# Layer 2's ends: where the recheck's branch stands, when rows are reloaded, and how far ahead pieces are requested

## The chip, the cores and the metric

The kernel runs on one core of a Trainium2 chip. The metric is device microseconds of one execution; a run's time is given beside the median of three runs. The profile is of one execution, taken by the hardware profiler. Its engines are PE (TensorE matmuls), PEld (TensorE weight loads), DVE (VectorE), ACT (ScalarE), POOL (GpSimd) and SP (SyncE, which here only issues DMAs and keeps order). PEclk is the TensorE clock that was granted, 1.00 being full speed.

## The reference

A graph network of four layers on 4096 nodes with 256 features and a random 0/1 adjacency `adj`; each layer is added to its input and normalised.

```python
x = ln(x + gat(x))                       # layer 0: attention over the edges, 8 heads
x = ln(x + (diag(adj) + adj) @ x @ W)    # layer 1
# layer 2, two steps on Xf = Xa = x:
R = rownorm(adj + eye)
for n in range(2):
    A = top_p_attention(Xa, p=0.9)       # softmax of q.k, only each row's nucleus, renormalised
    Xf, Xa = R @ Xf, A @ Xa
    Z = Z + Xf @ U1[n].T + Xa @ U2[n].T
x = ln(x + ln(x + Z) * g + b)
agg = adj @ x / max(deg, 1)              # layer 3
x = ln(x + relu(concat([x, agg]) @ W + b))
```

The nucleus of a row is the smallest set of its largest probabilities whose sum reaches 0.9. The layer's end in layer 2 holds two normalisations, one of its own and the residual one.

## The kernel before, in words

The 4096 nodes are 32 blocks (`NB`) of 128 rows. In layer 2 each of the two steps runs a loop over blocks 0 to 30, written out by hand (`tc.manual_schedule` keeps the order of the five engines as issued), with eight slots `s` in each block. A slot does one eighth of the block's attention product: `turn` (L1297, PE transposes of the masked scores), a copy to `aT` by ACT (L1299), and `gather` (L1306, eight matmul rows). Between the slots stand the pieces of other blocks' work: the scores of block b+2 (L935), DVE's nucleus of block b+1, and `diffusion`, the product R @ Xf of block b+2 (step 0) or b+3 (step 1). That product reads the adjacency in pieces of 256 KB, `adj_piece`, of which there are three buffers; SP requests them (L176) and PE multiplies each by the rows `XD` in four matmuls (L179). Every helper is a generator, and the loop's `next(...)` says where its next part goes.

When a step has no diffusion left (from block 30 in step 0, 29 in step 1), `XD` is no longer needed there. Then two things happen at the step's end:

- `reload` (L1153) brings the next operation's rows into `XD`, 1 MB for four blocks, on SP's queue. In step 0 these are the rows of the second diffusion, in step 1 the rows of layer 3.
- `early` (L1504 the matmuls, L1495 the piece's request) begins the next operation's products beside the last gathers: 21 pieces of blocks 0 to 2 in step 0, 35 pieces of blocks 0 to 4 of layer 3 in step 1. The order of the pieces is the list `todo`. In step 1 a piece on the diagonal gets the identity taken off by POOL (L1497). `made` records the products done.

A cheap nucleus is used, with a check: `settled` (L1186 to L1219) computes for each block whether the cheap cut was exact (`row`, with the minimum over all blocks as a flag); it ends in a DMA of `row` to memory (L1218, on SP's queue). Every engine loads the flag (`values_load`, L1690 in step 0, L1735 in step 1), and `mend` (L1155 to L1181) is a branch on it (L1159) whose body, the exact computation, is skipped here. In step 0 it stands in front of block 31's gather; in step 1 behind it, after the last `closing`'s first operation.

`store` (step 0) writes a block's result; `closing` (step 1, L1450 to L1467) scales it on ACT, adds the rest and runs both normalisations, mostly on POOL, and writes `xo`. `ahead3` (L1469) prepares the block's rows for layer 3 and writes them to `xtd`, from where `reload` takes them.

The tail of step 1, from block 31's gather on, holds the last closing, the reload of the last rows, the remaining pieces (`beside`), the last piece of each of the blocks 0 to 4, and `product(0..3)` (L1743), the whole product of block 5, whose pieces are casts into `kT` from the adjacency as bytes (`nad`, loaded by `load_bytes`, L1780, 1 MB a load). The bytes come in two sets of buffers: `nas` (in the score tiles `es[2]` and `es[0]`) and four tiles in `X`.

Layer 3 then goes over blocks 6 to 31. `ready(b)` casts the block's bytes to fp32r in eight-block pieces (`cast3`, L1790 on DVE, L1792 on ACT), `products(b)` is 32 matmuls (L1823), and `close(b)` (L1829 to L1839) is the mean, residual and normalisation. The six blocks that layer 2 began, `early3`, need only `close`.

## Time and profile before

| what | value |
|---|---|
| median of three runs | 4086.25 us (4081.27, 4086.25, 4087.33) |
| the profiled execution's own time | 4083.41 us |
| its span, first to last instruction | 4081.7 us |
| PE busy | 3911.8 us, 96% of the span |
| DVE busy | 2996.7 us, 73% |
| ACT busy | 2758.5 us, 68% |
| POOL busy | 1078.4 us, 26% |
| mean granted clock | 0.983 |
| last gather of step 1 done | 3832.1 us |
| last matmul of layer 2 done | 3872.2 us |

A timeline row gives the start, the length, the engine and line, the operation with its tiles, how many instructions were merged, and in brackets the engine's idle time before it with what released it. A row of waits gives the engine and line that waited, what it waited for, the sum in us, how often, and the longest. A "q" behind an engine's name is its sequencer. A window row gives the stretch, its length, then busy time of PE, PEld, DVE, ACT and POOL with the number of instructions, the granted clock, the busy share of the DMA engines and GB/s.

### The profile page before, as it was taken

The numbers are of one execution on the slowest core, as the hardware profiler recorded it, in microseconds if no ns is written. First come the engines' busy times: TensorE is split into PE (matmuls) and PEld (weight loads), VectorE is DVE, ScalarE is ACT, GpSimd is POOL, SyncE is SP. The second block draws the span as 40 slices with busy tenths as digits, with TensorE's granted clock in tenths as the row PEclk, the third lists the DMA queues.
The fourth block names the chain that finished last, engine by engine and source line by source line (L and its number), as shares of the span: only waits on it lengthen the run. The fifth ranks groups of instructions, "written<-read, shape, count | busy, mean of one in ns | idle before, by whom it ended". The sixth has DMA issues, their size and how long they took to land. (4 is left out here: it accounts for less than half of the span.)

```text
span 4081.7 us, 68719 instructions
## 1 busy us (share of the span) xinstructions
PE 3911.8 (96%) x25081; PEld 3381.4 (83%) x25081; DVE 2996.7 (73%) x6647; ACT 2758.5 (68%) x5127; POOL 1078.4 (26%) x1318
## 2 busy tenths in 40 slices
PE   7999989999999799799999999999999999999899
PEld 6899989999999688468888888865888888887677
DVE  7642329999999444548778787837899999999264
ACT  5543329999998322458888888825988888887132
POOL 0111110110333122301111111114555555555211
PEclk9999999999999999899999999999999999999999
DMA  4765555324221597433232332463333333335441
GB/s 119 230 211 176 179 178 186 96 85 143 76 89 43 205 380 281 120 106 99 97 102 92 100 97 95 140 196 99 109 108 103 118 103 105 119 100 204 163 150 47
DMA packets 291194, 555.90 MB, mean 136 GB/s; under 512 B 38966, under 2 KB 115382, under 8 KB 286742
## 3 DMA queue, kind: packets, MB, share of 16 engines
q1 hardware_dynamic: 208676, 394.61, 29.1%
q0 software_dynamic: 27664, 84.44, 6.2%
q10 hardware_dynamic: 54498, 72.27, 5.1%
q8 instruction: 203, 3.33, 0.3%
q14 instruction: 153, 1.25, 0.1%
HBM read 385.25 MB, written 165.94 MB: 135 GB/s over the span
## 5 line engine op out<-in xcount | busy, mean ns | idle before, releaser
L1306 PE MATMUL ps_a<-X,aT 128*128 128x256 f32 x4096 | 972.8, 380 | 1.3 <-ACT h L1447 1.1
L1306 PEld LDWEIGHTS ps_a<-X,aT 128*128 128x128 f32 x4096 | 775.8, 190 | 128.3 <-issue 3.6
L300 PE MATMUL acc<-gm,gt 128*128 128x198 bf16 x8192 | 704.2, 248 | 26.1 <-issue 14.9
L300 PEld LDWEIGHTS <-gt 128*128 128x128 fp8e4 x8192 | 700.3, 97 | 29.9 <-issue 15.1
L292 ACT ACTIVATE sg<-lpb,nlc 128x1024 fp8e4<-128x1024 f32 x640 | 671.4, 1135 | 59.6 <-DVE gt L294 34.4
L179 PE MATMUL ps_r<-XD,adj_piece 128*128 128x512 f32 x1952 | 548.5, 415 | 9.7 <-DMA adj_piece<-adjs 9.6
L517 PE MATMUL pz<-src,ar 128*128 128x264 f32 x4096 | 508.3, 287 | 11.9 <-DVE ar L507 9.8
L517 PEld LDWEIGHTS pz<-src,ar 128*128 128x128 f32 x4096 | 505.2, 189 | 14.8 <-DVE ar L507 13.6
L1028 ACT ACTIVATE ja<-e,nc 128x2048 uint8<-128x2048 f32 x240 | 480.9, 2004 | 2.0
L1299 ACT COPY aT<-ps_tp 128x512 f32<-128x512 f32 x512 | 296.4, 579 | 232.9 <-PE ps_tp L1297 230.8
L179 PEld LDWEIGHTS ps_r<-XD,adj_piece 128*128 128x128 f32 x1952 | 345.2, 189 | 85.4 <-DMA adj_piece<-adjs 13.9
L510 ACT ACTIVATE nb<-a 128x512 uint8<-128x512 f32 x256 | 156.8, 630 | 292.2 <-DMA a<-in_adjt_dram 289.8
L1093 DVE MAX8 cand<-v 128x8 f32<-128x256 f32 x1024 | 347.2, 412 | 4.4
L1143 DVE SCALAR_TENSOR_TENSOR e<-e,edge 128x512 f32<-128x512 f32 x512 | 347.3, 749 | 2.2
L1297 PE MATMUL ps_tp<-ident,e 128*128 128x128 f32 x2048 | 308.8, 274 | 2.1 <-DVEq L1159 2.1
L1089 DVE SCALAR_TENSOR_TENSOR v<-e,hi 128x2048 f32<-128x2048 f32 x128 | 301.4, 2355 | 2.4
L1297 PEld LDWEIGHTS ps_tp<-ident,e 128*128 128x128 f32 x2048 | 257.8, 142 | 54.2 <-issue 3.7
L935 PE MATMUL ps_logit<-kT,q 128*128 128x512 f32 x1024 | 277.6, 413 | 9.9 <-DVE kT L893 5.7
L285 DVE TENSOR_SCALAR sg<-lpb,nlc 128x1024 fp8e4<-128x1024 f32 x384 | 283.0, 773 | 2.0
L937 ACT ACTIVATE e<-ps_logit 128x1024 f32<-128x1024 f32 x256 | 260.1, 1026 | 30.7 <-PE ps_logit L935 29.6
L507 DVE CAST ar<-a 128x1024 fp32r<-128x1024 f32 x128 | 88.7, 693 | 232.0 <-PE pz L517 231.9
L731 PE MATMUL ps_adj<-XD,adj_piece 128*128 128x512 f32 x1024 | 236.1, 391 | 0.0
(382 smaller groups left out, 5501.1 us busy)
## 6 DMA issues: line engine op xcount, KB each, us to landing
adj_piece<-adjs SPq DMA_DIRECT2D x552, 256.0 KB
a<-in_adjt_dram SPq DMA_DIRECT2D x256, 256.0 KB
adjs<-adj_piece SPq DMA_DIRECT2D x96, 512.0 KB
na<-nad SPq DMA_DIRECT2D x64, 512.0 KB
nad<-nb POOLq DMA_DIRECT2D x128, 128.0 KB, 3.4
lpb<-lpd POOLq DMA_DIRECT2D x32, 512.0 KB, 4.1
na<-nad ACTq DMA_DIRECT2D x16, 1024.0 KB
gmd<-gb ACTq DMA_DIRECT2D x64, 198.0 KB
```

What stands on the lines that cost most here:

```text
L179: nc.tensor.matmul(ps, a[:, k, :], rhs(jc).rearrange("p s d -> p (s d)"), start=(jc == 0), stop=(jc == self.NB - 1))
L285: nc.vector.tensor_scalar(sg[:, k, :], lpb, nlc[:, jc, h:h + 1], 2.0 ** -5, op0=ALU.is_ge, op1=ALU.mult, saturate=False)
L292: nc.scalar.activation(sg[:, k, :], lpb, AF.Sign, scale=-1.0, bias=nlc[:, jc, h:h + 1], saturate=False)
L300: nc.tensor.matmul(acc[:, q, :6 * C1], gt[:, k, q * P:(q + 1) * P], gm[:, jc, hh, :], start=(jc == 0 and q % 2 == 0), stop=(jc == NB - 1 a ...
L517: nc.tensor.matmul(pz[q][:, t, :W], ar[:, q, k, :], src[:, jc, t, s], start=(jc == 0 and s == 0), stop=(jc == NB - 1 and s == 1))
L1028: nc.scalar.activation(ja, e[:, s * HALF:(s + 1) * HALF], f, bias=nc1, accum_out=fs[:, i + s:i + s + 1])
L1089: nc.vector.scalar_tensor_tensor(v, ec, hi, ec, op0=ALU.is_lt, op1=ALU.mult, accum_out=sb[:, s:s + 1])
L1093: nc.vector.max(cand[:, 8 * j:8 * j + 8], v[:, k * 256:(k + 1) * 256])
L1143: nc.vector.scalar_tensor_tensor(ec, ec, edge[:, j:j + 1], ec, op0=ALU.is_ge, op1=ALU.mult)
L1297: nc.tensor.transpose(pt[:, k * P:(k + 1) * P], e[:, jc * P:(jc + 1) * P], self.ident)
L1299: nc.scalar.copy(aT, pt)
L1306: nc.tensor.matmul(pa[:, :D], aT[:, k * P:(k + 1) * P], X[:, jc, :], start=(jc == 0), stop=(jc == NB - 1))
```

## The change

There are five parts.

1. In step 1 the branch (`values_load` of the flag and `mend`) stands in front of block 31's gather, as in step 0, and both steps share the code. `closing` loses its parameter `hand`. So that the row is there, the last parts of `settled` and of block 31's nucleus come in slots 6 and 7 of block 30, not after the loop. The row's DMA goes to ACT's queue. In step 0 the rest of blocks 0 to 2 of the next diffusion (last reload, last pieces, `diffused`, `keep`) follows the branch in the code; in the built order two of its three piece requests move behind the branch on SP, its reload does not.
2. The reloads of `XD` are given a slot each, by the table `freed` (key: block counted from the end of diffusion, slot): in step 0 slots 4 to 7 of the last block with diffusion and slots 0, 2 and 4 of the next; in step 1 over three blocks. Before, five came in slots 3 to 7 of one block (in step 1 in its slots with a piece), one or two straight behind it and one, in step 1, a block later.
3. `early` holds two requested pieces, not one, and requests the first two straight behind the last diffusion.
4. In step 1 the tiles `nas` are made and their four loads asked for behind the branch. The two of them into `es[0]`, which stood in front of the branch in the built order, move behind it; the two into `es[2]` stand in front of it in both. The four loads into `X`, which `ready(8)` asks for in the code of before and which stand amid the tail's pieces in its built order, are requested behind the last piece (`load_bytes(rows, 1, 0)`); `reload(xtd, NB - 4, NB - 1)` comes behind `whole(beside)`.
5. In layer 3 the casts of blocks 6 and 7 come first, and the six early closes are spread, one behind each of `products(6)` to `products(11)`, in the order 2, 5, 0, 1, 3, 4.

```diff
-            def mend(step, row, flag, e, r, h=None, made=()):
-
-
-                spare = es[(NB - 2 + step) % 3][:, :N]
+            def mend(step, row, flag, e, r, made=()):
+
+
+                spare = es[(NB - 2) % 3][:, :N]
                 with tc.If(flag == 0):
...
                     with tc.If(nc.values_load(row[:, NB - 1:NB], min_val=0, max_val=1) == 0):
-                        if step == 1:
-                            e2, Z = exact_scores(NB - 1, spare)
-                            r2 = exact_nucleus(e2, Z)
-                            nc.scalar.mul(h[:, 0], attention(e2)[:, :D], r2)
-                        else:
-                            e2, Z = exact_scores(NB - 1, e)
-                            nc.vector.tensor_copy(r, exact_nucleus(e2, Z))
+                        e2, Z = exact_scores(NB - 1, e)
+                        nc.vector.tensor_copy(r, exact_nucleus(e2, Z))
                     if step == 1:
...
                 nc.vector.tensor_reduce(row[:, NB:], pt[:1, :NB], AX.X, ALU.min)
-                nc.sync.dma_start(rowd, row)
+                nc.scalar.dma_start(rowd, row)
                 return rowd
...
-            def closing(b, pa, r, xb, hand=None, queue=nc.scalar):
+            def closing(b, pa, r, xb, queue=nc.scalar):
...
                 nc.scalar.mul(hb, pa[:, :D], r)
-                if hand:
-                    hand(h)
-                    yield
                 nc.gpsimd.tensor_add(hb, hb, xb[:, 0])
...
-                a = piece(step, *todo[0])
+                held = [piece(step, *t) for t in todo[:2]]
+                yield
                 started = set()
                 for i, (b, g) in enumerate(todo):
-                    after = piece(step, *todo[i + 1]) if i + 1 < len(todo) else None
-                    times(banks[b], a, g, b not in started)
+                    if i + 2 < len(todo):
+                        held.append(piece(step, *todo[i + 2]))
+                    times(banks[b], held.pop(0), g, b not in started)
                     made.append((banks[b], b, g, b not in started))
                     started.add(b)
-                    a = after
                     yield
...
                 banks, made = {}, []
+                freed = ((-1, 4), (-1, 5), (-1, 6), (-1, 7), (0, 0), (0, 2), (0, 4)) if step == 0 else \
+                    ((0, 4), (-1, 5), (-1, 6), (-1, 7), (0, 0), (0, 2), (1, 1))
+                freed = {at: g for g, at in enumerate(freed)}
                 if step == 0:
...
                             beside = diffusion(step, b + dd)
-                        elif b + dd == NB:
-                            beside = early(step, todo, banks, made)
                         if step == 0 and not ahead:
...
                             pieces = (1, 2, 2, 2, 2, 2, 1, 1)
-                        close, kept, put, difs, count = None, None, None, None, 0
+                        close, kept, put, difs = None, None, None, None
                         for s in range(8):
...
                                 next(beside)
-                                if b + dd == NB - 1 and count > 2:
-                                    reload(rows_of, 4 * count - 12, 4 * count - 8)
-                                count += 1
+                            if (b + dd - NB, s) in freed:
+                                g = freed[b + dd - NB, s]
+                                reload(rows_of, 4 * g, 4 * g + 4)
                             gather(pa, aTs.pop(0), s)
...
                                 aTs.append(turn(es[(b + 1) % 3], s - 6))
-                            if s == 1 and step == 1 and not ahead:
-                                reload(rows_of, NB - 8, NB - 4)
+                            if s > 5 and not ahead:
+                                if s == 6:
+                                    next(row)
+                                    next(edge)
+                                else:
+                                    row = result(row)
+                                    rs[b + 1] = whole(edge)
                         if b + dd < NB:
...
                         if b + dd == NB - 1:
-                            reload(rows_of, NB - 12, NB - 8 + 4 * (step == 0))
+                            beside = early(step, todo, banks, made)
+                            next(beside)
...
                         banks.update({3: pl[:, 0], 4: pl[:, 1]})
-                    next(row)
-                    next(edge)
-                    next(beside)
-                    row = result(row)
-                    rs[b] = whole(edge)
-                    for _ in range(3 if step == 0 else 5):
-                        next(beside)
+                    r = rs.pop(b)
                     if step == 0:
-                        reload(rows_of, NB - 4, NB)
-                        sums = [base(1, 0), base(1, 1)]
-                        for k in range(3):
-                            times(banks[k], piece(0, k, 7), 7)
-                            if k == 2:
-                                sums.append(base(1, 2))
-                            whole(diffused(1, k, banks[k], sums[k]))
-                            whole(keep(1, k, sums[k]))
-
-                r = rs.pop(b)
+                        store(b - 1, pa, rs.pop(b - 1))
+                        whole(beside)
+                    else:
+                        close = closing(b - 1, pa, rs.pop(b - 1), xc)
+                        next(close)
+                        for _ in range(6):
+                            next(beside)
+
+                flag = nc.values_load(row[:, NB:], min_val=0, max_val=1)
+                mend(step, row, flag, es[b % 3][:, :N], r, made[:] if step else ())
                 if step == 0:
-                    flag = nc.values_load(row[:, NB:], min_val=0, max_val=1)
-                    store(b - 1, pa, rs.pop(b - 1))
-                    mend(step, row, flag, es[b % 3][:, :N], r)
+                    reload(rows_of, NB - 4, NB)
+                    sums = [base(1, 0), base(1, 1)]
+                    for k in range(3):
+                        times(banks[k], piece(0, k, 7), 7)
+                        if k == 2:
+                            sums.append(base(1, 2))
+                        whole(diffused(1, k, banks[k], sums[k]))
+                        whole(keep(1, k, sums[k]))
                     pa = ps1.tile([P, 512], F32, name="ps_a")
...
-                nas = [t[:, i * 2048:(i + 1) * 2048].bitcast(U8).rearrange("p (k i) -> p k i", k=8)
-                       for t in (es[2], es[0]) for i in range(2)]
                 with tc.manual_schedule(engines=five):
+                    nas = [t[:, i * 2048:(i + 1) * 2048].bitcast(U8).rearrange("p (k i) -> p k i", k=8)
+                           for t in (es[2], es[0]) for i in range(2)]
                     self.load_bytes(nas, 0, 0)
                     xb = bases(b)
-                    close = closing(b - 1, pa, rs.pop(b - 1), xc)
-                    next(close)
                     h = done.pop(b - 2)
...
                             xT = turned(h[:, 0], bank())
-                    hand = []
-                    close = closing(b, pa, r, xb, hand.append)
-                    next(close)
-                flag = nc.values_load(row[:, NB:], min_val=0, max_val=1)
-                mend(step, row, flag, None, None, *hand, made[:])
-                with tc.manual_schedule(engines=five):
+                    close = closing(b, pa, r, xb)
                     ps = ps1.tile([P, 512], F32, name="ps_a")
...
                         next(beside)
-                    reload(xtd, NB - 4, NB - 1)
                     next(close)
                     whole(beside)
+                    reload(xtd, NB - 4, NB - 1)
                     lasts = []
...
                         lasts += [two[:, 0], two[:, 1]]
+                    rows = [X[:, 8 * i:8 * i + 8, :].rearrange("p b d -> p (b d)").bitcast(U8)
+                            .rearrange("p (k i) -> p k i", k=8) for i in range(4)]
                     product(0)
...
                         nc.tensor.matmul(to, t, XD[:, b].rearrange("p s d -> p (s d)"), start=False, stop=True)
-                self.ahead3 = nas, [X[:, 8 * i:8 * i + 8, :].rearrange("p b d -> p (b d)").bitcast(U8)
-                                    .rearrange("p (k i) -> p k i", k=8) for i in range(4)]
+                    self.load_bytes(rows, 1, 0)
+                self.ahead3 = nas, rows
                 self.early3 = [banks[k] for k in range(5)] + [ps]
...
                 it = b * P // self.IT
-                if b * P % self.IT == 0:
+                if b * P % self.IT == 0 and it > 1:
                     self.load_bytes(nas[it % 2], it, 0)
...
             ready(6)
-            for b, ps in enumerate(self.early3):
-                if b == 5:
-                    ready(7)
-                close(b, ps)
+            ready(7)
+            rest = [2, 5, 0, 1, 3, 4]
             for b in range(6, NB):
...
                     ready(b + 2)
+                if rest:
+                    k = rest.pop(0)
+                    close(k, self.early3[k])
                 close(b, ps)
```

## The prediction

> **What bounds the kernel now.** I read the table of windows first, because a share over the whole span mixes stages; it gives each stretch's length, the busy time of PE, PEld, DVE, ACT and POOL, the granted clock, the DMA share and GB/s.
>
> ```profile
> 2695.00:2712.00 17.00, 11.26 (x37) 8.17 (x38) 3.79 (x12) 2.44 (x4) 2.75 (x4) 0.70 0.52 171
> 3200.00:3600.00 400.00, 400.00 (x1972) 332.36 (x1971) 384.08 (x957) 351.90 (x842) 223.90 (x263) 1.00 0.34 110
> 3715.00:3732.00 17.00, 14.21 (x63) 11.13 (x62) 13.92 (x31) 10.22 (x31) 3.18 (x6) 0.90 0.96 362
> 3762.00:3795.00 33.00, 28.87 (x129) 23.05 (x128) 25.07 (x80) 4.45 (x9) 16.07 (x19) 0.90 0.59 191
> 3830.00:3855.00 25.00, 14.71 (x48) 10.22 (x47) 1.22 (x4) 4.37 (x5) 6.27 (x9) 0.83 0.76 265
> ```
>
> In the middle of step 1 PE is busy 400.00 of 400 us at clock 1.00, with DVE close behind (384.08). There nothing can be won, and the change leaves it alone. At the ends PE has holes and the clock falls: 11.26 busy of 17 at 0.70, 14.71 of 25 at 0.83. So the change can win at most those holes and the half-clock work after them.
>
> Next the early products' own line, with what ended PE's idle time before it, then PE's timeline at the holes (start, length, matmuls in the row, idle before and its releaser).
>
> ```profile
>   DMA adj_piece<-adjs: 40.0, 27
>   POOL adj_piece L1497: 11.0, 4
> ```
> ```profile
> 2698.81 1.43 PE L1504 MATMUL ps_logit<-XD,adj_piece 128*128 128x512 f32 x4 [2.79 <-DMA adj_piece<-adjs]
> 2700.03 1.91 PE L1504 MATMUL ps_r<-XD,adj_piece 128*128 128x512 f32 x4
> 2704.01 0.66 PE L1297 MATMUL ps_tp<-ident,e 128*128 128x128 f32 x2 [2.07 <-DVEq L1159]
> 3726.95 3.54 PE L1306 MATMUL ps_a<-X,aT 128*128 128x256 f32 x8
> 3773.78 1.65 PE L1504 MATMUL ps_logit<-XD,adj_piece 128*128 128x512 f32 x3 [3.07 <-POOL adj_piece L1497]
> 3840.20 3.44 PE L1504 MATMUL ps_logit<-XD,adj_piece 128*128 128x512 f32 x8 [4.62 <-DMA adj_piece<-adjs]
> 3848.40 1.20 PE L1504 MATMUL ps_logit<-XD,adj_piece 128*128 128x512 f32 x4 [1.86 <-DMA adj_piece<-adjs]
> 3874.08 11.44 PE L1823 MATMUL ps_tp<-XD,adj_piece 128*128 128x512 f32 x48 [1.88 <-DVE adj_piece L1790]
> ```
>
> Pieces that land late are the largest cause. Eight gather matmuls take 1.89 us elsewhere (the row at 3721.29) and 3.54 at 3726.95: a hole costs twice, once idle and once at half clock.
>
> Last, SP's waits near the end of step 1 (total, times, longest), and who waited for the branch in both steps:
>
> ```profile
> SPq L1495 <- PE ps_logit L1504: 52.3, 27, 5.9
> SPq L1159 <- SPq L1159: 19.1, 6, 6.5
> SPq L1218 <- DVE row L1217: 5.8, 1, 5.8
> ```
> ```profile
>   POOL h L1458: 13.1, 1
>   DVE v L848: 5.8, 1
>   PE ps_tp L1297: 2.1, 1
> ```
>
> SP, which alone requests pieces, stands in PE's shadow (a buffer must come free) and for 19.1 us in the branch. The branch costs PE 2.1 us in step 0, but POOL 13.1, which is idle time off the path.
>
> **The change, part by part.** The sum is made against the profiled run, 4083.41 us (span 4081.7). The median, 4086.25, is 2.84 above it; I take the saving off the median.
>
> *End of step 0* (reloads spread, pieces two ahead). PE waits for pieces at 2643.28, 2653.44, 2663.05, 2698.81 and 2705.56: 1.23 + 2.17 + 0.60 + 2.79 + 0.88 = 7.67. Half clock after them, from rows such as 1.91 against 1.18 for four matmuls: 2.8. Gross 10.5. In before, five 1 MB reloads go out in one block, on the queue of the pieces. A piece issued alone is used about 2.4 us after its issue, one behind a reload 5 to 7 (issued 3845.07, used 3852.42). With one reload every two slots (about 7 us, while 1 MB moves in some 3 to 4 at 265 to 362 GB/s) the queue should empty between. A reload can still hit one piece, and SP now requests the last two pieces behind the branch, not in front of it (2.4 us bare at worst, turns beside it): I keep back 1.5. The branch stays at its place, its 2.07 with it. **Net 9.0**, bounds 4 (the stalls of the first two rows only move) and 12 (the join shrinks too).
>
> *Blocks 28 to 30 of step 1* (the same, and two ahead). Idle 0.22 + 0.27 + 2.30 + 1.06 + 3.07 = 6.92; half clock 3.54 − 1.89 = 1.65, then 3.37 − 1.89 = 1.48 at 3775, and 0.7 at 3773.78, together 3.83. Gross 10.75. Of it the 3.07 is POOL: its diagonal addition L1497 (0.45) stood behind L1462 of the layernorm (2.75). A piece requested one earlier passes POOL before that. I keep back 1.75. **Net 9.0**, bounds 4 and 10.75.
>
> With three buffers the request of a piece waits in either kernel for the release of the piece three before it. So "two ahead" moves its place in the queues of SP and POOL, and hides no more than that. That is the ground of the first rival.
>
> *Mask, row and branch of step 1 in front of the gather.* Removed: idle 0.80 (3800.14) and 2.05 (3803.15, POOL's addition taking 2.84 beside DVE instead of 0.46), and half clock 2.9 behind them (eight transposes, four weighted products, a piece): 5.7. Added: a join of five engines with work left on PE. It queues PE's 64 gather matmuls with their transposes, ACT's copies aT and POOL's layernorm behind it, and two 1 MB loads of bytes on SP. Step 0 has that join and PE paid 2.07. Row and flag come by the same chain: the store of row, about 1 us to the loads (2695.72 to 2696.8), a load of 0.46 to 1.95, a branch of 0.05 to 0.07. Before it the last six pieces of `early` give PE some 5.6 us of cover (24 matmuls at 0.235); without them the chain's 3 to 4 us would be bare. The row's store on ACT's queue frees SP from 4.3 and 5.8 us of waiting; I credit it inside these terms. **Net 3.0**, nearest to step 0's row; bounds 0 and 5.
>
> *Tail, last gather to layer 3.* Before: gather done at 3832.1, layer 2's last matmul at 3872.2: 40.1 us. Idle 0.45 + 4.62 + 0.24 + 0.30 + 1.86 + 2.82 + 1.33 + 0.77 = 12.39; half clock 3.26 (3.44 − 2.12, 2.08 − 1.19, 3.14 − 2.09). Together 15.65; the rest, 24.4, is work. The cause: 4 MB of bytes for X are requested amid the pieces, between 3834.6 and 3859.2, and all SP work starts only when it leaves the branch at 3834.5. After, the branch is past and the X loads come behind the last piece. Two pieces fewer are left (8 matmuls, 1.9 us), but that work is only moved and counts for nothing. What is late next: the reload of 0.75 MB and the last pieces behind it, 3 us, which I keep back with 0.15 for the rest. **Net 12.5**, bounds 8 (pieces at the one-queue cadence of 2.4 us each) and 15.65.
>
> *Start of layer 3.* Idle 1.88 + 0.77 + 2.96 = 5.61 (casts behind closes) and half clock 9.27 − 7.47 = 1.8; gross 7.4. Two casts first remove the later two; the first cast still waits for the last block's xo store (issued 3869.92, cast at 3873.29), and the X loads now move beside it: keep 3.4. The closes, one per block, cost DVE about 2.7 each: 4.0 + 2.7 = 6.7 of 7.47 us per block, so they hide; uncovered, six would be 16. **Net 4.0**, bounds 1 and 5.
>
> Sum 9.0 + 9.0 + 3.0 + 12.5 + 4.0 = 37.5. One tenth (3.5) goes for stalls that no row of before shows: **34**, bounds 17 and 48. 4086.25 − 34 = **4052 us**; the ends are 4069 and 4038.
>
> **A rule against the rows.** Half clock makes 2.8 + 3.8 + 2.9 + 3.3 + 1.8 = 14.6 of my gross sum. The trace has it after single holes of 2.30 (3726.95) and 2.79 us (2700.03). The Trainium skill, "TensorE: Matmul & The Clock Gate", "Why this matters for your kernels", warns only of gaps over about 3 us. By it, only what follows the 3.07 and 4.62 holes would be throttled, 0.7 + 1.48 + 1.32 = 3.5, and the saving would be some 11 us smaller, about 23. The rows decide here.
>
> Moving the row's store to ACT's queue meets another one. The Trainium skill, "DMA: Bandwidth & Descriptors", "Issuing engines are not separate DMA queues", says that another issuing engine saves only issue time. By it this edit is worth next to nothing; SP's 5.8 us row is waiting and not transfer, so the two are not in conflict.
>
> **The rivals.** *Transfers bind still* (0.22): L1495's 52.3 us on PE in 27 waits says that a buffer, not the order, releases requests, and 362 GB/s at share 0.96 in the window at 3715 says that bytes limit there. Then each end keeps its bytes and stalls only move. Saved: 3 of step 0, 3 of blocks 28 to 30, 1.5 at the branch, 7.5 in the tail (X loads out of the way), 4 in layer 3: 19, so **4067**. Against it: the window after that one runs at 0.48.
>
> *The join holds all engines* (0.11): SP sat in step 1's branch from 3815.1 to 3834.6, 19.5 us. If that is the join's own price, and PE pays it now in both steps with 5 us half clock each, 2 × 24.5 = 49 stands against 34: +15, **4101**. It decides from 17 us of join per step. Against it: the last engine arrived at 3832.1 (ACT) and SP left 2.4 us later, so SP was waiting for the others.
>
> *Savings are given back* (0.07): the four X loads, now last, reach layer 3 late; 8 blocks' casts wait 4 us each, 32 of the 34 lost: **4084**. Against it: block 8, the first to use X, lies two blocks of 7.47 us behind the first product.
>
> **How the numbers follow.** Forecast 0.60, rivals 0.22, 0.11 and 0.07. A measurement of this kernel can tell about 0.2% (8 us) from no change. Forecast and the first rival lie wholly beyond that: faster 0.82; the third is within it: 0.07; the second slower: 0.11. The range 4038 to 4072 takes the forecast's bounds and the first rival with 5 us to spare, and leaves out 0.18.
>
> **What would show it.** Right: windows at both ends with PE over 95% busy and clock over 0.95; L1504's successor (L1496) waiting under 20 us for pieces and POOL; from the last gather to layer 3 about 26 us; the branch's PE wait under 3 us in both steps; the first layer 3 rows without holes after the first. Wrong: a PE idle of over 5 us released by the branch's engines, pieces still at 5 to 7 us between issue and use, or DVE as the releaser of PE in blocks 6 to 11 of layer 3. If the time falls and the holes stay, my places are wrong though the sum is not.

## The result and the profile after

The changed kernel took 4073.24 us (median of 7, 4066.64 to 4075.74) beside 4083.97 us of the kernel before (median of 7, 4081.27 to 4087.33). The ratio is 0.9971, 95% interval 0.9959 to 0.9983: faster, by 11 us and not by 34. Another five runs on a later occasion gave 4067.74, beside 4083.31 of before. The time lies above the range's upper end, 4072; the sign was right and the size was not.

The table of windows of the changed kernel, at the stretches shown of before and at the one that now holds the branch (length; busy PE, PEld, DVE, ACT, POOL; clock, DMA share, GB/s):

```profile
2695.00:2712.00 17.00, 13.34 (x60) 9.66 (x59) 4.98 (x14) 2.22 (x4) 1.02 (x2) 1.00 0.66 206
3762.00:3795.00 33.00, 32.88 (x159) 26.68 (x158) 30.00 (x88) 6.80 (x17) 15.43 (x20) 1.00 0.55 182
3795.00:3812.00 17.00, 11.23 (x37) 7.52 (x36) 3.40 (x8) 2.02 (x4) 5.96 (x7) 0.81 0.51 162
3830.00:3855.00 25.00, 18.66 (x65) 12.41 (x63) 1.22 (x4) 4.26 (x5) 6.29 (x9) 0.90 0.59 181
```

Block 30 of step 1 is full (32.88 of 33). The window with the branch is emptier than it was (11.23 of 17 at 0.81; before 14.15 at 0.80), and the tail is better but still a hole (18.66 of 25). What PE waited for in front of the early products, then PE's timeline at the holes that are left:

```profile
  DMA adj_piece<-adjs: 34.6, 27
  POOLq L1159: 4.3, 2
```
```profile
2673.24 1.20 PE L1496 MATMUL ps_logit<-XD,adj_piece 128*128 128x512 f32 x4 [1.79 <-DMA adj_piece<-adjs]
2686.89 2.07 PE L1496 MATMUL ps_logit<-XD,adj_piece 128*128 128x512 f32 x4 [3.22 <-DMA adj_piece<-adjs]
2704.52 2.11 PE L1496 MATMUL ps_logit<-XD,adj_piece 128*128 128x512 f32 x8 [2.85 <-DMA adj_piece<-adjs]
3798.77 4.62 PE L1496 MATMUL ps_logit<-XD,adj_piece 128*128 128x512 f32 x12 [1.95 <-POOLq L1159]
3808.32 0.41 PE L1385 MATMUL ps_tp<-ident,h 128*128 128x128 f32 x2 [3.52 <-PEq L1159]
3848.59 0.96 PE L1496 MATMUL ps_logit<-XD,adj_piece 128*128 128x512 f32 x3 [2.31 <-DMA adj_piece<-adjs]
3869.48 16.71 PE L1817 MATMUL ps_tp<-XD,adj_piece 128*128 128x512 f32 x64 [1.95 <-DVE adj_piece L1784]
```

The waits for pieces fell from 40.0 to 34.6 only. In step 0 each of the three holes stands behind one reload: these are the rows of the reloads on SP's queue, and the piece behind each starts on PE 6 to 9 us later.

```profile
2666.89 0.43 SPq L1153 DMA_DIRECT2D XD<-xfd  x1
2678.88 1.40 SPq L1153 DMA_DIRECT2D XD<-xfd  x1
2695.43 0.38 SPq L1153 DMA_DIRECT2D XD<-xfd  x1
```

The 3.52 us at 3808.32 are new. The 1.95 at 3798.77 are not: before, PE waited 2.05 us for POOL at the same point of the program (3803.15), and the forecast took that wait to go. Layer 3's first row now runs 64 matmuls without a hole, where before there were holes of 0.77 and 2.96 us in its first blocks.

Last, the branch itself, before and after (PE's sequencer is listed under PEld; the three numbers are the shortest, the median and the longest in ns), and SP's waits near the end of step 1:

```profile
L1159 PEldq COMPARE_BRANCH  x2: 359/1834/3308, 2701.8 to 3828.2; - x2
L1159 PEldq COMPARE_BRANCH  x2: 359/1984/3608, 2705.9 to 3804.3; - x2
```
```profile
SPq L1487 <- PE ps_logit L1496: 57.4, 24, 22.7
SPq L1159 <- SPq L1159: 2.2, 3, 1.1
```

PE's branch takes 0.36 us in one step and 3.61 in the other. SP no longer stands in the branch (2.2 us, before 19.1), but it still stands behind PE for its buffers (57.4, before 52.3). One wait of 22.7 us is new in that sum: it lasts through block 31's gather, in which PE uses no piece and so frees no buffer.

Executions of one kernel scatter by some us, much of it in stretches that the change does not touch: the trace of the changed kernel is 3.6 us later than that of before already at block 29 of step 0, and over all eighteen profiles that point lies between 2624 and 2643 us. So kernels are compared below by five stretches, worked out from the starts of PE's rows in each trace: **S0**, from block 29's first gather matmul to block 31's last in step 0; **B**, block 28's first to block 31's first in step 1, with the branch where it stands in front of the gather; **G**, block 31's gather; **T**, from its end to layer 3's first matmul; **L**, layer 3's first eight blocks. Each number is of one profile.

| us | S0 | B | G | T | L | time, median |
|---|---|---|---|---|---|---|
| before | 117.2 | 112.3 | 22.9 | 42.0 | 65.6 | 4083.97 |
| changed | 116.0 | 109.3 | 18.8 | 37.6 | 61.4 | 4073.24 |
| changed, again | 113.2 | 107.9 | 18.8 | 37.3 | 61.3 | 4067.74 |

Over the runs that do not touch a stretch, S0 lies at 113 to 116, B at 107.6 to 109.3, T at 35.9 to 38.1, L at 59.8 to 62.4. The stretches gain 17 and 21 us in these two profiles against the one of before; the medians gain 11 and 16. PE stands idle for 39 us of the five stretches before and for 27 in both profiles of the changed kernel; the rest of the gain, 5 and 9 us, is half clock.

### The profile page after: what moved, and what is told of

Same layout as the page of the kernel before. It is cut to its first block, busy times and chain, and to the rows that moved or that the text cites. A ratio compares the mean times of both kernels' runs of the same rounds, so it can differ in the third digit from the quotient of the medians.

```text
span 4072.8 us, 68706 instructions
## 1 busy us (share of the span) xinstructions
PE 3910.6 (96%) x25081; PEld 3381.8 (83%) x25081; DVE 2994.7 (74%) x6647; ACT 2755.4 (68%) x5127; POOL 1073.3 (26%) x1318
## 5 line engine op out<-in xcount | busy, mean ns | idle before, releaser
L517 PEld LDWEIGHTS pz<-src,ar 128*128 128x128 f32 x4096 | 507.2, 190 | 13.2 <-DVE ar L507 12.5
L1143 DVE SCALAR_TENSOR_TENSOR e<-e,edge 128x512 f32<-128x512 f32 x512 | 347.2, 750 | 2.2
```

What stands on the lines that cost most here:

```text
L517: nc.tensor.matmul(pz[q][:, t, :W], ar[:, q, k, :], src[:, jc, t, s], start=(jc == 0 and s == 0), stop=(jc == NB - 1 and s == 1))
L1143: nc.vector.scalar_tensor_tensor(ec, ec, edge[:, j:j + 1], ec, op0=ALU.is_ge, op1=ALU.mult)
```

## The experiments

Times are medians; the interval is of the ratio to the kernel before. Each edit is made to the changed kernel.

**The changed kernel again** (no edit).

> The changed kernel itself, unaltered, beside the others on one chip. Theory: the stretches in which it differs from the kernel before repeat within 1 us (last two blocks of step 0 to the second block of step 1: the end of step 0 gains only 1 to 2 us; blocks 28 to 31 of step 1 7; tail 4.4; first eight blocks of layer 3 4.3), and what differed elsewhere (3.6 us in front of the end of step 0, 4.3 at the start of step 1) is scatter between executions and does not repeat. Rival: the 4.3 us at the start of step 1 repeat and are a cost of the change. Time 4067 to 4074.

4067.74 us, 0.9950 to 0.9981. T, G and L repeated within 0.3 us, S0 within 2.8 and B within 1.4, not within 1; the 4.3 us at the start of step 1 did not: from the last gather of step 0 to block 28 of step 1 it took 951.2 us, 952.1 before and 956.4 in the first profile. The rival falls. The 3.6 us in front of block 29 of step 0 did not go, they were 6.2 here; with the spread given above they say nothing of the change.

### The branch

**A shorter body to jump over.**

```diff
-                mend(step, row, flag, es[b % 3][:, :N], r, made[:] if step else ())
+                mend(step, row, flag, es[b % 3][:, :N], r, ())
```

> The changed kernel, except that the skipped body of the recheck leaves out the redoing of layer 3's 28 early pieces in step 1 (never executed with these inputs; it only shortens the code that the branch jumps over). Theory (length of the jump): PE's own branch row takes 3.61 us in step 1 and 0.36 in step 0 of the changed kernel, because the body jumped over is longer there. Then it falls under 1 us, PE's idle of 3.52 us behind the branch falls to about 1, and the kernel is 3 to 5 us faster than the changed one (about 4069). Rival (the join): PE waits for another engine there; the 3.5 us and the branch row stay, and the time stays within 1 us of 4073.

4065.39 us, 0.9936 to 0.9968. The row of the branch, and what PE waited there:

```profile
L1159 PEldq COMPARE_BRANCH  x2: 339/348/358, 2705.9 to 3800.8; - x2
3801.58 0.41 PE L1385 MATMUL ps_tp<-ident,h 128*128 128x128 f32 x2 [0.81 <-PEq L1159]
```

3.61 became 0.36, 3.52 became 0.81, B is 105.7. PE is the last engine at the branch in both kernels (3800.8 against 3799.0 of SP, 3804.3 against 3803.8), so it waits for no other there; only skipped code went. The rival falls.

**A prefetch hint for the branch.**

```diff
-                with tc.If(flag == 0):
+                with tc.If(flag == 0, label=f"mend{step}"):
...
+                    tc.mark_branch_hint_location(f"mend{step}", "LikelyTaken", [ET.PE, ET.DVE, ET.SP])
                     b = NB - 1
```

> The changed kernel with a prefetch hint for the recheck's branch on PE, DVE and SP (it stands at the head of the code block in which the branch lies, some hundreds of us ahead of it in step 1). Theory (PE's 3.6 us at step 1's branch are the fetch of code behind a long jump): if the hint holds until then, PE's branch row falls from 3.6 us to under 1 and PE's idle of 3.5 to 4.2 behind it to about 1, as with the shorter body, 3 us faster than the changed kernel; if another jump or the distance voids it, nothing changes. Rival (a meeting of the engines): no change whether the hint holds or not.

4063.5 us, 0.9935 to 0.9966; B 104.9, and the whole body is kept:

```profile
L1159 PEldq COMPARE_BRANCH  x2: 354/367/380, 2700.6 to 3793.9; - x2
3794.74 0.41 PE L1385 MATMUL ps_tp<-ident,h 128*128 128x128 f32 x2 [0.85 <-PEq L1159]
```

PE executes the hint at 2701.6. The row thus depends on the length of the body and on the hint, and not on another engine: the 3.6 us are the fetch of the code behind the jump. The Trainium skill, "Runtime: NRT & Kernel Launch", "Instruction fetch mechanics", says that prefetch is sequential and that a taken branch to code outside the window at hand must fetch it first; it gives no time, and these rows agree with it.

**The branch behind the gather again** (`mend` and `closing` with `hand`, as before).

> The changed kernel with step 1's branch behind block 31's gather again, all else as changed (the loads into es[0] stand in front of it again, the row is still computed in block 30). Theory (in front of the gather PE pays 3.5 to 4.2 us for the branch and its half clock, and behind it the gather covered them, but SP's pieces and X loads wait for it there): blocks 28 to 31 become 4 to 5 us shorter, the tail 3 to 6 us longer, and the sum stays within 2 us of the changed kernel. Rival (the branch's place gave the tail's gain, as forecast): 6 us or more slower, all in the tail.

4066.6 us, 0.9939 to 0.9970. B is 103.0, T 37.8. PE's branch row still says 3348 ns, but PE waits 0.45 us:

```profile
3825.03 3.05 PE L1504 MATMUL ps_logit<-XD,adj_piece 128*128 128x512 f32 x12 [0.45 <-PEq L1159]
```

The first half of the theory held (5 us less in B), the second did not: the tail is not longer. Moving the branch gave the tail nothing and cost 5 to 6 us (B 107.9 and 109.3). The row of 3.3 us stood in the profile of before, hidden by the queued gather.

**Block 30's closing behind the six pieces.**

```diff
-                        close = closing(b - 1, pa, rs.pop(b - 1), xc)
-                        next(close)
                         for _ in range(6):
                             next(beside)
+                        close = closing(b - 1, pa, rs.pop(b - 1), xc)
+                        next(close)
```

> The changed kernel, but in step 1 the closing of block 30 is begun behind the six early pieces in front of the branch, not before them. Theory (POOL's order): the piece's diagonal addition on POOL then no longer stands behind the closing's first addition, which waits for ACT, which waits for the row's DMA; PE's wait of 1.95 us there goes, and 1.9 us of half clock behind it: 3 to 4 us faster than the changed kernel. Rival (the wait is the engines' meeting at the branch): it stays at its place or moves to PE's branch, and the time stays within 1 us.

4067.04 us, 0.9935 to 0.9969; B 107.4. PE's wait fell only from 1.95 to 1.27, and B is at the edge of its scatter: at most 1 us of the 3 to 4. The theory is not borne out. With the closing's addition out of the way, POOL's addition on the piece itself takes 2.20 us, 0.45 in the changed kernel.

**The row's store on SP's queue** (`nc.sync.dma_start(rowd, row)`).

> The changed kernel with the row's store on SP's queue again. Theory (ACT waits 5.8 us for the row, and with it block 30's closing, POOL's addition and PE's next piece, 1.95 us): on SP those go, but SP's next piece waits for the row instead; blocks 28 to 30 change by less than 2 us either way. Rival (freeing SP was a gain): 3 us or more longer.

4072.36 us, 0.9972 (0.9960 to 0.9985). B is 108.6, unchanged, but not for the theory's reason: ACT no longer waits for the row, and PE's wait at the piece is still there.

```profile
3795.36 3.07 PE L1496 MATMUL ps_logit<-XD,adj_piece 128*128 128x512 f32 x12 [2.11 <-POOL adj_piece L1489]
3791.67 3.06 POOL L1450 TENSOR_TENSOR h<-h,xb 128x256 f32<-128x256 f32 x1 [0.48 <-ACT h L1449]
```

So ACT's wait for the row is not its cause. What these kernels share is a POOL addition beside DVE's last four mask operations (L1143, 2.72 us together): it takes 2.84 us before, 2.05 in the changed kernel, 2.20 with the closing moved and 3.06 here, and each time it ends 0.3 to 0.6 us behind DVE's. The same two additions take as little as 0.45 and 0.73 us. That DVE's masks hold it up is read from these rows; no run moved them. S0 is 118.8, 3 to 6 us longer: PE waits 1.78 us for DVE at step 0's branch (0.30 in the changed kernel, 2.07 before), and its longest wait for a piece is 4.33 (3.22). In step 0 the move thus looks like a gain, by one profile.

### Reloads and pieces

**Reloads in one block again** (an approximation of the old places).

```diff
-                freed = ((-1, 4), (-1, 5), (-1, 6), (-1, 7), (0, 0), (0, 2), (0, 4)) if step == 0 else \
-                    ((0, 4), (-1, 5), (-1, 6), (-1, 7), (0, 0), (0, 2), (1, 1))
+                freed = {(-1, 4): (0, 1), (-1, 5): (2,), (-1, 6): (3, 4), (-1, 7): (5, 6)} if step == 0 else \
+                    {(-1, 4): (0,), (-1, 5): (1, 2), (-1, 6): (3,), (-1, 7): (4, 5), (1, 1): (6,)}
...
```

> The changed kernel with the reloads of rows back in one block of each step (step 0: two, one, two and two in slots 4 to 7 of block 29; step 1: one, two, one and two in slots 4 to 7 of block 28, one in block 30), all else as changed. Theory (each 1 MB in front of a piece costs PE a wait of its own wherever it stands): spreading moved step 0's waits and took few away, so step 0's end is within 2 us of the changed kernel's; in step 1, where a gather of blocks with DVE work stands between, it gave about 5 us, which are lost again. Rival (spreading lets the queue empty, as forecast): step 0 loses 6 us or more, step 1 8 or more.

4073.25 us, 0.9963 to 0.9983. The profiled execution is the slowest of the nine, 4087.69 us, so its stretches are read with care. S0 is 116.2, no more than with spread reloads. B is 116.0: 7 us lost in step 1, most of it in one hole and the half clock behind it:

```profile
3739.39 2.07 PE L179 MATMUL ps_r<-XD,adj_piece 128*128 128x512 f32 x4 [4.85 <-DMA adj_piece<-adjs]
3741.26 3.61 PE L1301 MATMUL ps_a<-X,aT 128*128 128x256 f32 x8
```

**Four reloads of step 0 left out** (the second diffusion's early products use old rows).

```diff
-                                reload(rows_of, 4 * g, 4 * g + 4)
+                                if step == 1 or b + dd < NB:
+                                    reload(rows_of, 4 * g, 4 * g + 4)
...
-                    reload(rows_of, NB - 4, NB)
```

> The changed kernel without the last four reloads of rows in step 0 (three in block 30 and the one behind the branch), so that the second diffusion's early products use old rows. Theory (the reloads in front of the pieces cause step 0's waits): the waits of 1.6 to 3.6 us for pieces there, about 7.5 in sum, and the half clock behind them go; the stretch of blocks 29 and 30 falls from 78 to 70 to 72 us. Rival (three buffers' round trips cause them, reloads or not): the stretch stays over 76 us.

4058.0 us, 0.9921 to 0.9954. S0 is 107.6; every wait for a piece in blocks 29 and 30 is gone but one of 1.09 us at the branch. (Of the 6 to 8 us, 3 to 5 came in blocks 29 and 30, which took 74.1 us and not 70 to 72, and 3 in block 31, which begins with the last pieces.) The rival falls. The forecast's 9 us were thus the price of reloads that cost nothing.

**Reloads in halves.**

```diff
-                            for _ in range(pieces[s]):
-                                next(beside)
+                            for i in range(max(pieces[s], 1)):
+                                if i < pieces[s]:
+                                    next(beside)
+                                if owed:
+                                    k = owed.pop(0)
+                                    reload(rows_of, k, k + 2)
...
-                                reload(rows_of, 4 * g, 4 * g + 4)
+                                owed += [4 * g, 4 * g + 2]
...
```

> The changed kernel, but each 1 MB reload of rows is cut into two of 512 KB, one of them behind each piece that is requested. Theory (one large transfer in front of a piece on the same queue is longer than three buffers cover): in step 0 the waits of 1.79, 3.22 and 2.85 us, each behind one reload, fall to under 3 in sum with the half clock behind the 3.22 gone, 5 to 9 us in all. Rival (bytes bind these blocks, whatever the order): the waits only change places, the sum stays over 6 us and the time within 2 us of 4073.

4065.32 us, 0.9938 to 0.9973. S0 110.9: waits of 2.05, 1.08, 0.74, 0.80, 0.17 and 0.69 us, 5.5 in sum and not under 3, but no row behind them is slow. In step 1 it cost a new hole of 2.32 (B 111.1).

**Step 0's reloads on ACT's queue** (`nc.scalar` where the rows are `xfd`).

> The changed kernel with step 0's reloads of rows requested by ACT, so that they stand on another queue than the pieces. Theory (order on one queue): pieces no longer wait for the whole of a reload, the stretch of blocks 29 and 30 falls to 72 to 75 us, unless ACT, which must wait for the rows to be released, holds up its copies of aT. Rival (bytes: the queues share the DMA engines): the stretch stays within 1 us of 78.

4070.53 us, 0.9956 to 0.9981. S0 115.4: within its scatter. Waits of 1.65, 0.32, 1.14, 2.50, 2.77 and 1.13 us stayed. Blocks 29 and 30 took 81.3 us, 2 to 4 more than in the changed kernel, so both views missed. The order on one queue is not enough of a cause: with a megabyte on the way beside them the pieces were late from either queue, which speaks for its bytes. When ACT issued each reload was not held equal.

**One piece requested ahead.**

```diff
-                held = [piece(step, *t) for t in todo[:2]]
+                held = [piece(step, *t) for t in todo[:1]]
...
-                    if i + 2 < len(todo):
-                        held.append(piece(step, *todo[i + 2]))
+                    if i + 1 < len(todo):
+                        held.append(piece(step, *todo[i + 1]))
```

> The changed kernel with early holding one requested piece and not two. Theory (three buffers bind, so that a request leaves when PE has used the piece three before, whichever number is held): PE's waits for pieces in both ends stay within 2 us in sum, and the time within 2 us of the changed kernel. Rival (two ahead was a gain by itself): 4 us or more slower, in new waits for pieces and for POOL's diagonal additions.

4071.74 us, 0.9965 to 0.9987. My theory (and the first rival of the forecast) fell: B is 115.6, 7 us longer, by POOL, whose addition then stands behind the layernorm again.

```profile
3764.20 1.65 PE L1496 MATMUL ps_logit<-XD,adj_piece 128*128 128x512 f32 x3 [4.61 <-POOL adj_piece L1489]
```

S0 is 111.5, 2 to 4 us shorter. Two ahead pays in step 1 and costs in step 0; why it costs there stays open.

### Tail and layer 3

**Tail pieces requested during the last gather, into kT.**

```diff
...
+                        slot = kT[:, 512 * g:512 * g + 512].rearrange("p (k i) -> p k i", k=4)
+                        if g < 5:
+                            extra.append(piece(1, *todo[len(made) + 2 + g], slot))
+                        else:
+                            sevens.append(piece(1, g - 5, 7, slot))
...
-                        held.append(piece(step, *todo[i + 2]))
+                        held.append(extra.pop(0) if extra else piece(step, *todo[i + 2]))
...
```

> The changed kernel, but eight of the pieces used behind the last gather of step 1 are requested during that gather, into the free tile kT, instead of into the three piece buffers as they come free; the casts of block 5 come behind them. Theory (three buffers bind the tail: a request waits until PE has used the piece three before): PE's idle between the last gather and layer 3, 7.2 us for pieces, falls under 3, with 2 to 3 us less at half clock, and the stretch falls from 38 to 28 to 31 us; the kernel is 7 to 10 us faster than the changed one (about 4065). Rival (the last closing, or the bytes, bind the tail): the stretch stays over 35 us, PE's waits move to the casts, the closing or the reload.

4064.71 us, 0.9933 to 0.9965. T is 30.3, 7 us less. PE's waits between the gather and the last product are 3.08 and 0.81 us, 3.9 in sum and not under 3, in the changed kernel 7.2:

```profile
3835.95 4.71 PE L1496 MATMUL ps_logit<-XD,kT 128*128 128x512 f32 x20
3844.68 1.58 PE L1496 MATMUL ps_logit<-XD,adj_piece 128*128 128x512 f32 x4 [3.08 <-DMA adj_piece<-adjs]
```

The other 4 us are work at full clock (PE is busy for 24.3 us of T, in the changed kernel for 28.5 and 26.4). So the three buffers account for about half of what was won here, as waits, and the last closing binds at most the 0.81 us, which PE waits for its rows. That bytes do not is argued and not shown: the DMA share over the changed kernel's tail is 0.65, but the edit also moves 2 MB ahead of it.

**X loads in layer 3's code again.**

```diff
-                    self.load_bytes(rows, 1, 0)
...
-                if b * P % self.IT == 0 and it > 1:
+                if b * P % self.IT == 0:
```

> The changed kernel with the four 1 MB loads into X asked for in layer 3's code again, as before. Theory (they stood in front of the tail's pieces on one queue and cost 4 us of the tail): the tail grows by 3 to 6 us and layer 3's first blocks stay as they are. Rival (the tail is bound by the three buffers' round trips whatever else is loaded): the tail stays within 1 us; the rest of what was gained there came from the branch's move.

4065.31 us, 0.9935 to 0.9968. Both views fell: T is 33.8, nearly 4 us *shorter*. With the branch out of the way, the built order puts these loads behind the branch and one piece, and SP issues them from 3813 to 3828, during the gather, when it has nothing else to do. So they do not stand among the tail's pieces. The 4 us themselves are not waits, which are 8.0 us in sum against 7.2. They are the clock, as the windows of T show, of the changed kernel first:

```profile
3831.87:3869.49 37.62, 28.48 (x95) 19.17 (x94) 2.99 (x9) 6.01 (x9) 6.29 (x9) 0.86 0.65 228
3827.92:3861.76 33.84, 24.17 (x95) 16.62 (x94) 2.98 (x9) 5.82 (x9) 6.26 (x9) 1.00 0.50 160
```

The same matmuls take 28.48 us at 0.86 and 24.17 at 1.00. Whether the loads' place did that is not shown; T's clock was 0.86 to 0.94 in the kernels that do not touch it.

**Closes in front of block 7's casts again.**

```diff
-            ready(7)
-            rest = [2, 5, 0, 1, 3, 4]
+            for b, ps in enumerate(self.early3):
+                if b == 5:
+                    ready(7)
+                close(b, ps)
+            rest = []
```

> The changed kernel with layer 3's early closes in front of block 7's casts again, as before. Theory (the casts behind the closes made PE wait): layer 3's first eight blocks take 65 to 66 us and not 60 to 62, 3.5 to 5 us slower. Rival (the casts wait for the loads and stores at that moment, not for the closes): 62 us or less, within 1 us of the changed kernel.

4071.72 us, 0.9960 to 0.9983. L is 63.9, 2.5 us longer, in one hole of 2.24 us in front of the third product. It lies between the two views: about 2.5 of the 4.3 us are the casts' order, as far as one profile tells; where the rest came from was not tried.

### Together

**Hint, slots, step 0's reloads in halves, X loads in layer 3's code.**

> The changed kernel with the hint, eight tail pieces requested during the last gather into kT, step 0's reloads in 512 KB parts and the X loads in layer 3's code. Theory (each part's stretch gain adds up: tail 7 us, step 0's end 3 to 4, the branch 3 if the hint holds, X loads 1 to 3 as the tail is already shorter): 10 to 15 us faster than the changed kernel, 4053 to 4060. Rival (the X loads now stand in front of the eight pieces and give the tail's gain back): 4062 or more.

4055.25 us (5 runs, 4051.88 to 4063.67), 0.9934 (0.9920 to 0.9947): faster than both. S0 110.5, B 104.8, T 32.7, L 59.8. S0 and B kept their gains; T is 2.4 longer than with the slots alone, in waits (3.05 and 3.54 us for pieces), so the X loads, which now stand in the gather beside the eight pieces, seem to have taken part of it, as the rival said; its time of 4062 or more did not come.

**The same with the branch behind the gather and no hint.**

> As the last one, but without the hint and with step 1's branch behind the gather. Theory: the branch is then covered by the gather (4 us less in blocks 28 to 31), but the pieces for the tail are requested in front of it and land in time, so the tail keeps most of its gain: within 3 us of the last one, 4055 to 4062. Rival (SP stands in the branch until all engines have come, and everything behind it is late): the tail is longer than 38 us and the time over 4065.

4057.91 us (5 runs), the same ratio and interval. S0 110.8, B 103.5, T 32.4. The branch's place does not make the tail longer here either, though PE waits 2.64 us for SP's branch in it, and the gather hides the fetch as well as the hint does.

## Why the prediction was wrong, step by step

| term | forecast | measured |
|---|---|---|
| end of step 0 | 9.0 | 1 to 4 (S0) |
| blocks 28 to 30 | 9.0 | 10 and 11 (first gather matmul of 28 to the last of 30: 101.2 before, 90.9 and 89.9) |
| branch in front of the gather | 3.0 | minus 3 (from there to the end of block 31's gather: 33.9 before, 37.2 and 36.9; 31.0 with the branch behind it) |
| tail | 12.5 | 4.4 to 4.7 (T) |
| start of layer 3 | 4.0 | 4.3 (L) |

Three terms failed, the tail by 8 us, the end of step 0 by 5 to 8 and the branch by 6. The 4067.74 of the second occasion lies inside the range, but the tail and the branch missed by as much there.

**End of step 0.** The failed step is that with one reload every two slots "the queue should empty between". I kept back 1.5 us for one hit; three were hit, for 1.79, 3.22 and 2.85 us. Without four of the reloads the forecast gain is there (S0 107.6). With them each megabyte costs step 0 a wait wherever it stands, and on either queue; in halves it costs less. Why a megabyte does so, by its bytes or by the three buffers, stays open.

**Blocks 28 to 30.** Right. Without spreading or without two ahead 6 to 7 us of it are lost (97.3 and 96.9). "Hides no more than that" was too cold on two ahead: its place in POOL's queue was the gain, as the term itself said of the 3.07.

**The branch.** The failed step is the price of the join. I took PE's 2.07 us of step 0 and "a branch of 0.05 to 0.07", from rows of the other engines. PE's own row in that view read 359/1834/3308: 3.3 us in step 1, hidden by a gather that was queued ahead of it. The change took that cover away, and the question "what hides it now" was asked of the flag's chain but not of the branch instruction. The wait for POOL, 2.05 us, was counted as removed and stayed (1.95): the additions still stand beside DVE's last masks.

**Tail.** The holes were there, but I gave them to the X loads' place among the pieces and SP's time in the branch. SP's time in the branch was not it: with the branch back T is 37.8. And with the X loads asked for in layer 3's code, PE's waits in T are 8.0 us, hardly more than 7.2. With three buffers a request waits until PE frees one, and PE then waits for the piece: eight more places took the 7.2 us to 3.9. The SP row of 52.3 us on PE, quoted for the rival, said so. The half clock in the tail, 3.3 us by the forecast, did not go either: PE is busy for 27.7 us of T before and for 28.5 and 26.4 after. The lower bound of 8 rested on the same cadence and was still too high. The two pieces by which the forecast thought the tail shorter are not gone; it has as many matmuls as before. Which part of the change took its 4.4 us stays open: neither the branch's old place nor the X loads' gave them back alone, and both together were run with the slots only.

**Start of layer 3.** Right in size; the casts' order is 2.5 of it.

**Half clock.** Its size in before was read rightly. An estimate from busy time of PE, against profiles in which the same stretch ran at clock 1.00 (S0 106.2 against 103.2, B with G 125.2 against 118.1, T 27.7 against 24.2, L 61.9 against 59.8), gives 16 us beside the forecast's 14.6. The failed step is that it goes with the holes that were seen: by the same estimate 11 us are left in the changed kernel and 6 when it ran again, behind the holes that stayed and the new ones. Nor does a hole have one price. The same hole of 1.95 us in front of the same 12 matmuls was followed by 4.62 us for them in the changed kernel and by 3.08 when it ran again:

```profile
3792.20 3.08 PE L1496 MATMUL ps_logit<-XD,adj_piece 128*128 128x512 f32 x12 [1.95 <-POOLq L1159]
```

Of the rivals, the first was nearest: a buffer, not the order, releases requests, and step 0's and the tail's holes moved. Its condition, two ahead brings nothing, was wrong. The second, a join that costs 19.5 us, was far off; at the join PE paid 3.5 and 4.2 us, and not through the other engines.

## What to carry to other kernels

Before a branch, or any instruction of an engine's sequencer, is moved, read its own duration on each engine in each place, and ask which queued work covers it; a skipped body can cost the length of a fetch, and a hint or a queue of ready matmuls hides it. Where requests wait for a buffer, reordering them moves holes; more room during an idle stretch of the queue, here a tile that was free during the last gather, takes part of them away. Price a large transfer beside small urgent ones at one wait each, and try it in parts: in step 0 halves gained 2 to 5 us, in step 1 they cost a new hole. Read how much of a gain is idle time and how much is clock, from busy time against the same work at clock 1.00; the clock's part did not repeat from one profile to the next.

## What the runs showed of the hardware that was not expected

- PE's branch over the recheck's body took 3.3 to 4.6 us in step 1 in fifteen profiles with the full body and no hint, 0.36 with a shorter body and 0.38 with a hint that stands right behind step 0's branch, 1,090 us ahead; on the other engines the branch row stayed at 45 to 84 ns.
- A hole of 1.95 us was followed by half clock in one execution and not in another of the same kernel. The Trainium skill, "TensorE: Matmul & The Clock Gate", "What's actually happening", says that the activity window runs freely and does not start with the work; the two rows, 4.62 and 3.08 us, agree with that.
- Moving a 1 MB reload to another engine's queue left the pieces' waits about as they were (9.5 us in sum against 8.5; S0 115.4 against 113 to 116).
- Two POOL additions that take as little as 0.45 and 0.73 us took 2.05 to 3.06 beside DVE's four masks of 2.72 us together, and ended 0.3 to 0.6 us behind them, in four kernels.
